# The last two recurrent steps of the last block, run in two halves of 256 positions with output rows beside the second half

## The chip, the cores and the metric

The kernel runs on one core of a Trainium2 chip. The metric is the device time of one execution in microseconds (us); the median of three runs before the change is 2809.48 us (2809.25 to 2809.84). Five engines work beside each other, each in the order of its own instruction list: PE multiplies matrices (PEld is its loading of weights), DVE, ACT and POOL work element by element, SP issues the DMA transfers. An engine whose next instruction waits does nothing else in the meantime.

## The reference

The input has 8 sequences of 2048 positions with 512 features. A long convolution with a residual comes first. Its result `x` then goes through a gated recurrence over the first axis: there are 8 steps, and the 2048 positions are the batch.

```
def step(c, xt):
    ft = sigmoid(xt @ wf.T + c @ uf.T + bf)
    it = sigmoid(xt @ wi.T + c @ ui.T + bi)
    gt = tanh(xt @ wc.T + c @ uc.T + bc)
    return ft * c + it * gt
c_final = scan(step, c0, x)                  # x: layer norm of the residual
h = tanh(x @ wo.T + c_final @ uo.T + bo)     # all 8 steps use the same c_final
out = x_residual + layernorm(h)
```

No output row of a position can be made before all 8 steps of that position are done, because `h` needs `c_final`. Different positions don't depend on each other.

## The kernel before, in words

**Tiles.** The 2048 positions are four blocks `q` of 512. A block is four chunks of 128 positions (`cj` 0 to 3). The products of a step are done by a scheme of Strassen's kind, with seven products of half blocks in place of eight: chunks 0 and 1 are one half of the positions, chunks 2 and 3 the other, and so a matmul has 256 moving columns (`BP`), of which the first 128 belong to chunks 0 and 2 and the last 128 to chunks 1 and 3. Numbers are split into a high and a low 16-bit part, and each product takes three matmuls.

**Units.** `part_a(key)` opens a unit: four accumulators of 256 columns in PSUM (pool `pu`, three buffers). It issues the products `FIRST` (24 matmuls with the input, then 24 with the state), and then ACT and DVE form sums of the accumulators in place (L993 to L997). `part_b(key)` adds the products `THEN` (18 and 18 matmuls), and ACT applies the gate's function (L1021). A step has two `z` units (the product of the input with `wo`, 24 and 18 matmuls, no state; stored to `z_d`, L1012 to L1014) and six gate units (three gates for each of two feature parts). All these matmuls are issued in `mms`, L955. When the third gate of a part is done, `state` (L1041 to L1047, DVE) makes the new state and `halves` (L1054 on ACT, L1056 on DVE) splits it into `cf`, which the next step's matmuls read.

**Order.** The order on each engine is written out by hand. A step is 16 places; its eight units go one after another, and each unit's closing part stands behind the opening part of the next. `put` files other work at places and `go` issues it there: `turn` reads the input rows of the next step, normalises them, transposes them on PE (L485) and splits them (L101, L102); `prep` makes the input of the next block; `head` makes the output rows of the block before, one every three places. A `head` loads `z` (a buffer of tag `zr`, of which there are four) and the residual row, adds the final product on POOL (L1128), applies tanh on ACT (L1131), takes statistics on DVE (L462 to L465), makes scale and offset by three small POOL instructions (L471 to L476), normalises on ACT (L1145), adds the residual on POOL (L1146) and stores. SP's list holds all loads and stores in the same hand-written order, so a load whose buffer is still in use holds up the ones behind it.

**The end.** The last block has no block after it. When its eighth step is done, the function `last` multiplies `c_final` with `uo` for its four chunks (`sums`, L450 to L452, 12, 12, 18 and 18 matmuls of 512 columns, two chunks in one PSUM tile) and adds the bias (L1098). Then 16 `tail` entries follow, each for one chunk and two steps: two additions on DVE (L1179), two tanh on ACT (L1180), statistics on DVE, the three small POOL instructions, two normalisations on ACT (L1187), and the residual additions on POOL (L1192; one in eight of them on DVE). Their loads reuse weight tiles and other tiles that the last step leaves.

Of the kernel before, what the change touches and what calls it, by code (L numbers as in the profile page):

```python
# [59 lines left out]
def s4_gated_block(ctx, tc, a, dbg=None):  # L60
# [888 lines left out]
    def mms(u, prods, w, x, opens, stop):  # L949
# [3 lines left out]
        for j, (f, b, d, k, i) in enumerate(n):  # L953
# [3 lines left out]
            seen.add(bank)  # L957

    def views(key):
        q, t, kind, n = key  # L960
        xf = xfs[q, t]
        if kind == "z":
            cs = slice(n * P, (n + 1) * P)
            return (lambda f, b, l, k: xf[:, b, int(l), k, cs], lambda f, b, l, k: wts[3][:, k, f, int(l)]), None
        ms = slice(n * P, (n + 1) * P)
        w, uw, cf = wts[kind], wts.get(4 + kind), cfs.get((q, t - 1))
        return ((lambda f, b, l, k: w[:, k, f, int(l), ms], lambda f, b, l, k: xf[:, b, int(l), k]),
                (lambda f, b, l, k: uw[:, k, f, int(l), ms], lambda f, b, l, k: cf[k][:, b, int(l)]))

# [4 lines left out]
    def part_a(key):  # L974

        q, t, kind, n = key
        z = kind == "z"
        u = units[key] = pu.tile([P, 4, BP], F32, name="u")
        for pr in FIRST:
            mms(u, places(key, pr), *views(key)[0], True, not t or z)  # L980
        if t and not z:
            mms(u, FIRST[0][:1] + FIRST[1] + FIRST[0][1:], *views(key)[1], False, True)
        if z:
            if n == 0:
                gates["z"] = FT.tile([P, 2, BP], F32, name="zc")
            c22 = gates["z"][:, n]
        else:
            g = gates[key] = FJ.tile([P, 4, BP], F32, name="gate2", tag="wq") if kind == 2 else FT.tile([P, 4, BP], F32, name=f"gate{kind}")
            c22 = g[:, 2]
        z_, v_ = (UV, UZ) if z else (UZ, UV)  # L990
        u2 = u2p[:, len(u2s) % 2]
        u2s.append(key)
        S.activation(u2, u[:, UX], AF.Copy)  # L993
        V.tensor_tensor(u2, u2, u[:, UY], ALU.add)  # L994
        V.tensor_tensor(c22, u2, u[:, z_], ALU.add)
        V.tensor_tensor(c22, c22, u[:, v_], ALU.add)
        V.tensor_tensor(u[:, 2:4], u[:, 2:4], u2[:, None].to_broadcast([P, 2, BP]), ALU.add)  # L997

    def part_b(key):

        q, t, kind, n = key
        u, z = units.pop(key), kind == "z"
# [22 lines left out]
        if kind == 2:  # L1025
            V.scalar_tensor_tensor(g, gates.pop((q, t, 1, n)), 1.0, g, ALU.add, ALU.mult)  # L1026
        elif kind == 0:
            return state(q, t, n)

    def state(q, t, n):  # L1030

        f, ig = gates.pop((q, t, 0, n)), gates.pop((q, t, 2, n))
        if t == 0:
            cds[q, n] = FT.tile([P, 4, BP], F32, name=f"cd{n}")
        cd = cds[q, n]
        for h in range(2):
# [12 lines left out]
        def halves():  # L1049
            cf = FT.tile([P, 7, 2, BP], F16, name=f"cf{n}", bufs=2 - n)  # L1050
            cfs.setdefault((q, t), []).append(cf)
            parts = ((0, cd[:, 0]), (slice(3, 5), ts[:, 0:2]), (slice(5, 7), ts[:, 2:4]), (slice(1, 3), cd[:, 2:4]))
            for fs, src in parts:
                S.activation(cf[:, fs, 0], src, AF.Copy)  # L1054
            for fs, src in parts:
                V.tensor_tensor(cf[:, fs, 1], src, cf[:, fs, 0], ALU.subtract)  # L1056
# [5 lines left out]
    def last(q):  # L1062
# [3 lines left out]
        def load():  # L1066
            if end:
                u4 = FE.tile([P, KT, 2, H], F16, name="uw", tag="xf")
                dma(out=u4, in_=uo_d.rearrange("k p a m -> p k a m"))
                uws.extend(u4[:, k] for k in range(KT))  # L1070
                return

            for i, (pool, tag) in enumerate(((FJ, "wl"), (FE, "y"))):
                u2 = pool.tile([P, 2, 2, H], F16, name="uw", tag=tag)
                dma(out=u2, in_=uo_d[2 * i : 2 * i + 2].rearrange("k p a m -> p k a m"))
                uws.extend(u2[:, k] for k in range(2))

        def load_b():
            bo = FE.tile([P, H], F32, name="bo", tag="xa", bufs=2) if end else FT.tile([P, H], F32, name="bo", tag="x1r", bufs=2)
            dma(out=bo, in_=a["bo"])  # L1080
            uws.append(bo)

        def sums(cj):
            cf, i, cs = cfs[q, NB - 1], cj // 2, slice(cj % 2 * P, (cj % 2 + 1) * P)
            if end and cj % 2:
                u = us[cj - 1]
            else:
                u = pu.tile([P, 4, BP], F32, name="u").rearrange("p (a b) c -> p a (b c)", a=2)
            us[cj] = u
            ps = [(k, b) for k in ((0, 2, 1, 3) if end else range(KT)) for b in (((FB11,) if i == 0 else (FB11, FT1)) if k < 2 else ((FB21,) if i == 0 else (FB22,)))]  # L1090
            for n, (k, b) in enumerate(ps):
                mm3(u[:, cj % 2], lambda l: cf[k % 2][:, b, l, cs], lambda l: uws[k][:, l],
                    start=(n == 0), stop=(n == len(ps) - 1))

        def out(cj):
            p_ = us[cj][:, cj % 2]
            if end:
                V.scalar_tensor_tensor(p_, uws[KT], SW, p_, ALU.mult, ALU.add)  # L1098
                us_[QC * q + cj] = p_
            else:  # L1100
# [15 lines left out]
    def head(q, cj, t):  # L1116
# [34 lines left out]
        return load, sum_, gate, stat, scale, load_x, out, store  # L1151

    def tail(q, cj, tp, n):

        c, s_ = QC * q + cj, {}

        def load():
            w = (3, 1, 5, 2, 6, 0)[n // 3]
            if n % 3 == 0:
                tails[w] = (FW if w < 2 else FV if w == 2 else FT).tile([P, 3, 2, H], F32, name="zz", tag=f"w{w}", bufs=1)  # L1160
            s_["z"] = tails[w][:, n % 3]
            dma(out=s_["z"], in_=z_d[c, :, 2 * tp : 2 * tp + 2])

        def load_x():
            i = (n + 3) % 9
            if n == 15:
                s_["x"] = tails[0][:, 1]
            elif i < 3:
                if i == 0:
                    tails[4] = FT.tile([P, 3, 2, H], F32, name="xw", tag="w4", bufs=1)  # L1170
                s_["x"] = tails[4][:, i]
            else:
                s_["x"] = (FJ, FJ, FE, FT, FJ, FT)[i - 3].tile([P, 2, H], F32, name="xx", tag=("wl", "ws", "y", "gate1", "wq", "gate0")[i - 3])
            dma(out=s_["x"], in_=x1_d[c, :, 2 * tp : 2 * tp + 2])
# [23 lines left out]

    tails = {}
    gsc = (0.5 / SW, 0.5 / SW, 1.0 / SW)  # L1200
    bias = FE.tile([P, 3, KT], F32, name="bias")
# [30 lines left out]
    end = last(NQB - 1)  # L1232
    rows = [tail(NQB - 1, cj, tp, 4 * cj + tp) for cj in range(QC) for tp in range(NB // 2)]

# [3 lines left out]
    for n, (q, t) in enumerate(steps):  # L1238
        b = 16 * n
        if q and t == 0:  # L1240
            put(last(q - 1), b, (-1, 4, 3, 5, 5, 7, 7, 9, 13, 14, 15))
        if n + 1 < len(steps):
            ps = ((2, 5, 6, 7, 8, 9), (9, 10, 11, 12, 13, 14)) if n else ((0, 1, 2, 3, 5, 6), (5, 6, 7, 8, 9, 10))
            for i in range(2):
                put(turn(*steps[n + 1], i), b, ps[i])
        if n == len(steps) - 1:
            put(end[:2], b, (2, 3))
            for i in range(3):
                put(rows[i][:2], b, (8 + 2 * i, 9 + 2 * i))
            for i in range(3, 9):  # L1250
                put(rows[i][:1], b, (13,))
        for (gp, cj), (n_, p) in zip(chunks, when):
            if n_ == n:
                put(prep(*pairs[gp], cj, (1, 0, 2)[cj] if n == 0 else 0), b, p)
        if q and t:
            for r in range(QC * NB):
                p = 3 * r + 17 - 16 * t
                if 0 <= p < 16:
                    put(head(q - 1, r // NB, r % NB), b, [p + d for d in (0, 2, 4, 6, 8, 9, 10, 12)])
    with tc.manual_schedule(engines=MAN | {mybir.EngineType.SP}):  # L1260
        before = None
        for n, (q, t) in enumerate(steps):
            zs = [(q, t, "z", i) for i in range(2)]
            gs = [(q, t, gt, mp) for mp in range(2) for gt in (1, 2, 0)]

            def finish(key, p):
                st_ = part_b(key)
                if st_:
                    put([st_], p, [1])

            for sl, key in enumerate(zs + gs if n else gs[:5] + zs + gs[5:]):
# [12 lines left out]
                go(p + 1)  # L1284
        part_b(before)
        for p in sorted(todo):
            go(p)
        for f in end[2:6]:
            f()
        for n in range(len(rows) + 5):  # L1290
            if n % 4 == 0 and n < len(rows):
                end[6 + n // 4]()
            for st_, d in ((0, -3), (1, -3), (6, 5), (2, 1), (3, 2), (4, 3), (5, 3)):
                if 0 <= n - d < len(rows) and (st_ > 1 or n - d > (2 if st_ else 8)):
                    rows[n - d][st_]()
# [62 lines left out]
```

## Time and profile before

| What | us |
|---|---|
| median of three runs | 2809.48 |
| profiled execution, its own time | 2808.14 |
| its span from first to last instruction | 2806.4 |
| PE busy in the span | 2552.5 (91%) |
| DVE busy | 2095.5 (75%) |
| ACT busy | 1480.0 (53%) |
| POOL busy | 1226.8 (44%) |
| last matmul of a gate issued, last block | 2724 |
| first statistics of a tail row | 2740.1 |
| last store issued | 2802.8 |

Busy shares are means over the whole span, in which stages with different limits follow each other: the convolution first, then four blocks of eight steps, then the tail. Where a row of the profile has a form such as `u<-xf,w`, the left side is the tile written and the right side the tiles read; `L955` is the line of the kernel that issued it. In a timeline the columns are start, duration, engine, line, operation, tiles, shape and how many instructions are merged. A chain of waits is read in order of time: each piece is what the next one was waiting for. PE works on several matmuls at once, so the time that matmuls take in a stream is the distance between their starts, not the duration shown for one.

### The profile page before, as it was taken

To read this page: it belongs to the slowest core of one execution; us is meant where nothing else is said; L and a number is where in the kernel's file an instruction comes from. 1 tells how busy PE (TensorE), PEld (TensorE's weight loads), DVE (VectorE), ACT (ScalarE), POOL (GpSimd) and SP (SyncE) were. 2 spreads that over 40 slices of the span, in tenths; PEclk is the share of its full clock that TensorE was granted. 3 is DMA by queue.
4 is the path that set the end of the run, shared out by engine and by line. 5 is a ranking of instruction groups with operands and counts; after the bars stand their busy time and mean duration, and the time that the engine had idled before them with its cause. 6 is when DMAs were issued, how large, how long until landed. Compare 5 with 4: busy or idle time off the path is not lost.

```text
span 2806.4 us, 60001 instructions
## 1 busy us (share of the span) xinstructions
PE 2552.5 (91%) x23940; PEld 2229.7 (79%) x23940; DVE 2095.5 (75%) x4248; ACT 1480.0 (53%) x3091; POOL 1226.8 (44%) x1520
## 2 busy tenths in 40 slices
PE   4578888896999999999999999999999999999991
PEld 3367777785888888788898887888898788888870
DVE  7878888867667766677887777778777677777748
ACT  8966666654444444445555444455555454554436
POOL 5777777743112211124554431355554224543307
PEclk9799999998999999999999999999999999999995
DMA  6977887887334433225564432356554234543356
GB/s 236 304 238 241 259 257 246 257 282 209 99 86 126 106 98 91 80 91 150 164 180 138 142 102 95 109 162 178 155 165 129 91 106 136 166 121 102 104 170 234
DMA packets 507536, 449.25 MB, mean 160 GB/s; under 512 B 275574, under 2 KB 386680, under 8 KB 502264
## 3 DMA queue, kind: packets, MB, share of 16 engines
q1 hardware_dynamic: 506824, 444.90, 52.7%
q8 instruction: 187, 3.06, 0.4%
q14 instruction: 93, 0.76, 0.1%
q10 hardware_dynamic: 432, 0.52, 0.1%
HBM read 293.58 MB, written 151.78 MB: 159 GB/s over the span
## 4 chain that ended last, share of the span: by engine, by line
PE 62%; DVE 7%; ACT 3%; issue 1%; POOL 1%; DMA 0%; SPq 0%; POOLq 0%; DVEq 0%; ACTq 0%
PE u L955 60%; PE pt L485 2%; DVE zz L1179 1%; ACT gate L1021 1%; DVE u L997 1%; DVE cd L1042 1%; DVE gate L1041 0%; DVE cf L1056 0%; DVE sth L462 0%; ACT xf L101 0%; DVE u2p L994 0%; DVE xf L102 0%; PE u L451 0%; ACT zr L1145 0%; ACT cf L1054 0%
## 5 line engine op out<-in xcount | busy, mean ns | idle before, releaser
L955 PEld LDWEIGHTS <-w 128*128 128x128 f16 x15120 | 1481.0, 98 | 198.9 <-issue 16.0
L955 PE MATMUL u<-xf,w 128*128 128x256 f16 x8064 | 944.2, 273 | 17.8 <-DVE u L997 6.1
L955 PE MATMUL u<-cf,w 128*128 128x256 f16 x7056 | 825.7, 273 | 2.0 <-DVE cf L1056 2.0
L1021 ACT ACTIVATE gate<-u,bias 128x512 f32<-128x512 f32 (+1 forms) x384 | 200.9, 574 | 275.2 <-PE u L955 274.9
L993 ACT ACTIVATE u2p<-u 128x256 f32<-128x256 f32 x256 | 96.6, 379 | 436.9 <-PE u L955 436.8
L955 PE MATMUL u<-w,xf 128*128 128x256 f16 x2688 | 310.5, 273 | 4.0 <-DVE u L997 4.0
L1146 POOL TENSOR_TENSOR x1r<-x1r,zr 128x512 f32<-128x512 f32 x96 | 133.4, 1390 | 410.5 <-ACT zr L1145 295.2
L994 DVE TENSOR_TENSOR u2p<-u2p,u 128x256 f32<-128x256 f32 x256 | 106.7, 417 | 267.3 <-ACT u2p L993 265.9
L909 POOL TENSOR_TENSOR xr<-y,xr 128x512 f32<-128x512 f32 x120 | 160.7, 1360 | 300.0 <-ACT y L908 300.0
L955 PEld LDWEIGHTS <-xf 128*128 128x128 f16 x2688 | 263.0, 98 | 36.3 <-DVE u L997 5.5
L997 DVE TENSOR_TENSOR u<-u,u2p 128x512 f32<-128x512 f32 x256 | 179.0, 699 | 8.7
L646 POOL TENSOR_TENSOR u<-xg,u 128x512 f16<-128x512 f32 x104 | 129.2, 1242 | 106.7 <-ACT u L644 105.6
L471 POOL TENSOR_TENSOR rsy<-rsy,nhalf 128x2 f32<-128x2 f32 (+1 forms) x68 | 51.0, 751 | 281.6 <-DVE rsy L465 280.6
L640 POOL TENSOR_TENSOR xg<-xg,mu 128x512 f32<-128x512 f32 x112 | 162.8, 1460 | 6.0 <-DMA xg<-in_xr 6.0
L102 DVE TENSOR_TENSOR x<-pxt,x 128x256 f16<-128x256 f32 x240 | 100.1, 419 | 63.6 <-ACT x L101 62.3
L1026 DVE SCALAR_TENSOR_TENSOR gate<-gate,gate 128x1024 f32<-128x1024 f32 x64 | 90.0, 1406 | 69.6 <-ACT gate L1021 68.5
L1128 POOL TENSOR_TENSOR zr<-zr,ur 128x512 f32<-128x512 f32 x96 | 130.0, 1354 | 21.1 <-DMA zr<-z_d 12.3
L666 PE MATMUL pxt<-x,at 128*128 128x256 f16 x224 | 61.9, 277 | 79.3 <-DVE x L102 78.9
L462 DVE BATCH_NORM_STATS2 sty<-y 128x6 f32<-128x512 f32 x120 | 76.9, 682 | 76.1 <-DMA y<-y_d 76.1
L101 ACT ACTIVATE x<-pxt 128x256 f16<-128x256 f32 x240 | 91.5, 382 | 73.5 <-PE pxt L666 67.8
L451 PE MATMUL pyt<-u,t 128*128 128x128 f16 (+2 forms) x544 | 123.7, 227 | 0.0
L452 PE MATMUL pyt<-u,t 128*128 128x128 f16 (+2 forms) x544 | 123.3, 227 | 0.0
(373 smaller groups left out, 5261.1 us busy)
## 6 DMA issues: line engine op xcount, KB each, us to landing
xs<-in_rr SPq DMA_DIRECT2D x32, 1024.0 KB, 6.4
t<-kpad SPq DMA_DIRECT2D x32, 1024.0 KB, 5.6
y_d<-y SPq DMA_DIRECT2D x30, 1024.0 KB, 7.6
xr<-in_r SPq DMA_DIRECT2D x60, 512.0 KB, 5.8
xa<-x_d SPq DMA_DIRECT2D x120, 256.0 KB, 4.0
y<-y_d SPq DMA_DIRECT2D x59, 512.0 KB, 5.8
x_d<-xr SPq DMA_DIRECT2D x59, 512.0 KB, 3.1
xg<-in_xr SPq DMA_DIRECT2D x28, 1024.0 KB, 8.6
```

Source lines behind the costliest of these rows:

```text
L102: V.tensor_tensor(lo, src, hi, ALU.subtract)
L451: T.matmul(out, lhsT=w(1), rhs=x(0), start=False, stop=False)
L452: T.matmul(out, lhsT=w(0), rhs=x(1), start=False, stop=stop)
L640: Q.tensor_tensor(xg, xg, bc(mu1), ALU.subtract)
L646: (V if g == 2 else Q).tensor_tensor(u[:, js, 1], xg, u[:, js, 0], ALU.subtract)
L909: Q.tensor_tensor(xv, yv, xv, ALU.add)
L955: T.matmul(u[:, d], lhsT=w(f, b, i == 1, k), rhs=x(f, b, i == 2, k), start=opens and bank not in seen, stop=stop and j == len(n) - 1, skip ...
L994: V.tensor_tensor(u2, u2, u[:, UY], ALU.add)
L997: V.tensor_tensor(u[:, 2:4], u[:, 2:4], u2[:, None].to_broadcast([P, 2, BP]), ALU.add)
L1021: act = lambda o, s_, b: S.activation(o, s_, AF.Tanh, scale=gsc[kind], bias=b)
L1128: Q.tensor_tensor(s_["z"], s_["z"], us_[c], ALU.add)
L1146: Q.tensor_tensor(s_["x"], s_["x"], s_["z"], ALU.add)
```

## The change

The six first steps of the last block, and everything before them, stay as they were, except for the places of the last `head` rows. For the last two steps (6 and 7):

- The gate units are split by columns into two halves of 128 (256 positions: chunks 0 and 2, then chunks 1 and 3). The order is step 6 of the first half, step 7 of the first half, step 6 of the second half, step 7 of the second half. The `z` units stay whole and stand at the four joints. A half unit has as many matmuls as a whole one, with 128 moving columns, and as many ACT and DVE instructions, on tiles half as wide.
- `part_a` is cut into `open_` (the input's matmuls) and `fill` (the state's matmuls and the sums). At three joints both first gate units are opened before the first is filled.
- The halves share `cf` tiles: the first half of step 6 writes a new tile for feature part 0 and the tile of step 5 for part 1, step 7 writes the tile of step 5.
- The output sums of chunks 0 and 2 stand in the second half's first step, and their result goes to SBUF (tile `ue`). Eight new `pair` entries make the output rows of these chunks beside the second half. They take `zr` buffers (two each; every third takes one tile `zp` instead), and sum and residual are added on POOL.
- Only the eight entries of chunks 1 and 3 remain in the `tail` after the last step. Their tiles, and those of `uw` and `bo`, are others than before.
- The `head` rows of the third block come every 2.5 places instead of every three.

```
+    def open_(key):
+        t, z = key[1], key[2] == "z"
+        u = units[key] = pu.tile([P, 4, BP], F32, name="u")[:, :, 0 : P if len(key) > 4 else BP]
+        for pr in FIRST:
+            mms(u, places(key, pr), *views(key)[0], True, not t or z)
+
+    def fill(key):
+        q, t, kind, n = key[:4]
+        z, u = kind == "z", units[key]
+        w = u.shape[-1]
         if t and not z:
             mms(u, FIRST[0][:1] + FIRST[1] + FIRST[0][1:], *views(key)[1], False, True)
...
+            if len(key) == 4 or t == NB - 2 and n == 0 and key[4] == 0:
+                cf = FT.tile([P, 7, 2, BP], F16, name=f"cf{n}", bufs=2 - n)
+            elif key[4] == 0:
+                cf = cfs[q, NB - 3][n]
+            else:
+                cf = cfs[q, t][n]
...
+    def pair(q, cj, tp, n):
+        c, s_ = QC * q + cj, {}
+
+        def load():
+            if n % 3 == 2:
+                z = FJ.tile([P, 2, H], F32, name="zp", tag="ws")
+                s_["z"] = [z[:, i] for i in range(2)]
+                dma(out=z, in_=z_d[c, :, 2 * tp : 2 * tp + 2])
+                return
+            s_["z"] = [FT.tile([P, H], F32, name="zr", bufs=4) for _ in range(2)]
+            for i in range(2):
+                dma(out=s_["z"][i], in_=z_d[c, :, 2 * tp + i])
+
+        def load_x():
+            s_["x"] = (FE, FJ)[n % 2].tile([P, 2, H], F32, name="xx", tag=("y", "wl")[n % 2])
+            dma(out=s_["x"], in_=x1_d[c, :, 2 * tp : 2 * tp + 2])
+
+        def sum_():
+            for z in s_["z"]:
+                Q.tensor_tensor(z, z, us_[c], ALU.add)
...
+        def out():
+            for i, z in enumerate(s_["z"]):
+                x = s_["x"][:, i]
+                Q.tensor_tensor(x, x, z, ALU.add)
...
-                p = 3 * r + 17 - 16 * t
+                p = (3 * r if q < NQB - 1 else (5 * r + 1) // 2) + 17 - 16 * t
...
+    SA, SB = 39, 47
+    put(end[:2], PL, (20, 30))
+    put((end[2], end[6]), PL, (SA, SA + 2))
+    put((end[4], end[8]), PL, (SB, SB + 1))
+    for i, r in enumerate(early_rows):
+        p0 = PL + SA + 3 + 3 * i
+        put(r, p0, ((-4 if i < 3 else -2), 0, 2, 3, 5, 3, 6, 7, 9))
+    for i, p in enumerate((50, 50, 50, 60, 60, 60, 61, 61)):
+        put(rows[i][:1], PL, (p,))
+    for i, p in enumerate((62, 61, 63, 63)):
+        put(rows[i][1:2], PL, (p,))
...
+        hs = [[(q, t, gt, mp, i) for mp in range(2) for gt in (1, 2, 0)] for i in range(2) for t in (NB - 2, NB - 1)]
+        zs = [(q, t, "z", i) for t in (NB - 2, NB - 1) for i in range(2)]
+        A, B = lambda k: [(part_a, k)], lambda k: [(finish, k)]
+        O, F = lambda k: [(open_, k)], lambda k: [(fill, k)]
+        run = lambda g: sum((A(g[k]) + B(g[k - 1]) for k in range(2, 6)), [])
+        first = lambda g: F(g[0]) + F(g[1]) + B(g[0])
+        two = lambda g: O(g[0]) + O(g[1])
+        plan = (A(zs[0]) + B(before) + A(zs[1]) + B(zs[0]) + two(hs[0]) + B(zs[1]) + first(hs[0]) + run(hs[0])
+                + A(zs[2]) + B(hs[0][5]) + B(zs[2]) + two(hs[1]) + first(hs[1]) + run(hs[1])
+                + A(hs[2][0]) + B(hs[1][5]) + A(hs[2][1]) + B(hs[2][0]) + run(hs[2])
+                + A(zs[3]) + B(hs[2][5]) + B(zs[3]) + two(hs[3]) + first(hs[3]) + run(hs[3]) + B(hs[3][5]))
+        for p, (f, key) in enumerate(plan):
+            f(key, PL + p) if f is finish else f(key)
+            go(PL + p)
```

In the list that `put` gets for a `pair`, the numbers are the places of load of `z`, sum, tanh, statistics, small POOL group, load of the residual, normalisation, residual addition and store, counted from the pair's own place; the places now are the 63 entries of `plan`, each some half as long as a place before. Input rows of step 7 (`turn`) stand at entries 1 to 17.

## The prediction

> **What bounds the kernel now.** I read the windows of the last 150 us first, then the chain that ended last, then the timeline at the places that the change touches. All times are microseconds from the span's start. First the windows (columns: stretch, length, busy time and count of PE, PEld, DVE, ACT, POOL, granted clock, DMA share, GB/s):
>
> ```profile
> 2440.00:2502.80 62.80, 62.80 (x578) 56.48 (x576) 49.47 (x98) 32.66 (x65) 30.92 (x42) 1.00 0.59 166
> ...
> 2660.00:2724.00 64.00, 64.00 (x589) 57.37 (x587) 33.57 (x63) 19.58 (x41) 8.86 (x14) 1.00 0.50 166
> 2724.00:2740.00 16.00, 11.80 (x42) 4.25 (x41) 9.37 (x16) 4.84 (x9) 0.00 (x0) 0.79 0.54 193
> 2740.00:2790.80 50.80, 4.68 (x22) 1.94 (x20) 49.60 (x106) 35.64 (x55) 42.57 (x62) 0.59 0.70 230
> 2790.80:2806.00 15.20, 0.00 (x0) 0.00 (x0) 6.60 (x12) 5.15 (x8) 11.46 (x14) 0.50 0.66 267
> ```
>
> Up to 2724 PE has no gap and everything else hides under it. From 2740 DVE is the bound (49.60 of 50.80) and POOL is close (42.57). The chain says the same, with the hand-over between:
>
> ```profile
> 2646.91 77.30 PE u L955 x708
> ...
> 2724.24 0.70 ACT gate L1021
> ...
> 2731.55 0.61 PE u L451
> ...
> 2736.95 0.71 DVE u L1098
> ...
> 2740.17 0.66 DVE sth L462 x2
> ...
> 2790.84 0.66 DVE sth L462 x2
> ```
>
> The reader is to see three prices: last gate matmul to first statistics 16 us; then one output pair after another, (2790.84 - 2740.17)/14 = 3.62 us each; then 15.6 us from the fifteenth pair's statistics to the end. So tail from first statistics to end is 2806.4 - 2740.1 = 66.3 us for 16 pairs. Of the last two steps, the first matmul (z unit of step 6) starts at 2590.0, which is where I start the sum.
>
> **The change, part by part.**
>
> *Tail.* Eight of 16 pairs leave it: 66.3 - 8 x 3.62 = 37.3 us from first statistics to the end. Gross gain 29 us. All else is what this costs.
>
> *Narrow matmuls.* 24 half units of 84 matmuls (2016, 128 moving columns) replace 12 units (1008, 256 columns at 109 ns, from 578 matmuls in 62.8 us). Nearest rows, convolution stage:
>
> ```profile
> 303.11 0.22 PE L450 MATMUL pyt<-u,t 128*128 128x128 f16 x1
> 303.16 0.23 PE L451 MATMUL pyt<-u,t 128*128 128x128 f16 x1
> 303.23 0.23 PE L452 MATMUL pyt<-u,t 128*128 128x128 f16 x1
> 303.29 0.22 PE L450 MATMUL pyt<-x,m 128*128 128x120 f16 x1
> 303.34 0.22 PE L451 MATMUL pyt<-x,m 128*128 128x120 f16 x1
> 303.39 0.22 PE L452 MATMUL pyt<-x,m 128*128 128x120 f16 x1
> ```
>
> Starts lie 50 to 70 ns apart for 128 columns with strided weights (mean 62; weight load 150 ns) and 52.5 ns for 120 columns with dense weights (weight load 98 ns, as in the gates). I scale the second to 128 columns: 56 ns, so 2016 x 56 - 1008 x 109 = +3 us; ends 0 (54.5 ns) and +15 (62 ns). The Trainium skill ("TensorE: Matmul & The Clock Gate", Back-to-back issue gap) gives about 81 ns for a sustained load-and-multiply pair at 128 columns; by that the estimate would be 2016 x 81 - 1008 x 109 = +53 us and the kernel 50 us slower than my sum. The rows above contradict it, and I go by them.
>
> *PE up to slot 42.* I call an entry of the new plan a slot (0 to 62). The first early pair's sum stands at slot 42. PE work from 2590.0 to there: closing part of the unit before 36 x 0.109 = 3.9; three z units 3 x 42 x 0.109 = 13.7; twelve half units 12 x 84 x 0.056 = 56.4; 300 of the 504 matmuls of the next half step, 300 x 0.056 = 16.8; two transposes of 0.87 = 1.7; output sums of chunk 0, 12 x 0.2155 = 2.6. Sum 95.2.
>
> *Waits that the change adds on PE there.* Order and cover change at the start of step 6. The second z unit closed after a full 5.2 us opening of the next gate; now only two half openings (2.7 us) stand ahead of it. What it waits for is DVE:
>
> ```profile
> 2603.30 0.68 DVE L1056 TENSOR_TENSOR cf<-cd,cf 128x512 f16<-128x512 f32 x1
> 2603.90 0.41 DVE L994 TENSOR_TENSOR u2p<-u2p,u 128x256 f32<-128x256 f32 x1
> ...
> 2605.26 0.70 DVE L997 TENSOR_TENSOR u<-u,u2p 128x512 f32<-128x512 f32 x1
> ```
>
> DVE is on the state and its halves until 2603.98, so that z unit's sums end at 2605.96, while PE would be there at 2603.8. The second opening takes the first z unit's PSUM buffer (three in all), which ACT empties only after the state's copies, about 2605.1. That is 2.6 us of idle PE. Behind it: statistics, POOL's three small instructions (1.2) and two norms (1.5) must come ahead of the moved transposes, and ACT's first copy of the next unit is queued behind them: 1.9 us more. At the next step boundary DVE has 2.3 us of input halves ahead of the z sums: 1.8 us. Sum 6.5 us; ends 0 (all other boundaries of the trace show none) and 10. SP's next input loads wait for the transposes, 20 us ahead of need. The remaining half units wait little: per half step DVE has 17.7 us (128-column operations at 0.28, 256 at 0.42, 512 at 0.69) against 27.5 us of PE, and the state chain of about 4.1 us is covered by 4.6 us of z and openings. No half unit waits for the other half's state in the compiled order. So slot 42 starts at 2590.0 + 95.2 + 6.5 = 2691.7.
>
> *Early pairs.* Each takes two sums and two outs on POOL, 1.28 each (row L1128 shows 1.35 in the mean), a small group of 1.2, two tanh and two norms on ACT, 2.25 of statistics on DVE, and on SP one or two z loads, an x load and a store. Slot 42 to the first out: units 2.7 + 2.0 + 2.7 + 2.0, z and a closing 2.6 + 2.0, sums of chunk 2 3.9, z closing 2.0, copies and norm 1.9: 21.8 us. From there a ring binds. The z buffers hold three pairs, so the load of pair i+3 waits in SP's queue for the out of pair i; its sum on POOL waits for that landing; and on POOL the out of pair i+1 stands behind that sum. One turn is out 2.55, issue 0.1, landing, sum 2.6. Landings:
>
> ```profile
> xa<-x_d SPq DMA_DIRECT2D x120, 256.0 KB, 4.0
> ...
> zr<-z_d SPq DMA_DIRECT2D x96, 256.0 KB, 4.4
> ...
> zz<-z_d SPq DMA_DIRECT2D x16, 512.0 KB, 6.2
> ```
>
> Five turns (outs 0 to 4, sums 3 to 7), one of them with a 512 KB load: 5 x 5.25 + 4 x 4.4 + 6.2 = 50.0. Ends: windows of 50 us show medians of 3.1 (xa) to 5.6 (zr) and 4.6 (xx) to 6.4, so 43 to 55. Pitch would be 10 us against 6 planned, and DVE has 43 us of work in PE's 48 us from slot 42 to 62, so nothing is caught up. While a sum is late, its tanh blocks ACT, and with it the gate copies, the state and PE (I find PE idle for some 9 us here, last gate matmul about 2749). That is no term: the ring ends later than PE.
>
> *Ring to tail.* Remaining pairs end ahead of the late ones on every queue. After the last sum: out 2.55, small group 1.2, norm 0.8, out 2.55, small group 1.2, two norms 1.6, then the late row's tanh 0.6, plus 1 for an x load behind a store: 11.5. Last output sums (24 matmuls, 0.43 cold or 0.22, about 8 us) and chunk 1's out on DVE lie beside that. Ends 8 (x early) and 14.
>
> *At no cost.* Uw and bo move to tiles that are free by then, and load 20 slots ahead of their use. The heads of the block before come every 2.5 slots instead of 3 in steps 25 to 29: PE is full there and DVE has 49.5 of 62.8, so some 2 us more of DVE a step hide; if not, 1 us a step. DVE and ACT have 78 and 64 more instructions in the compiled order, POOL 18, SP 6, all counted above. Late z loads are issued before PE ends, as now.
>
> *Sum.* 2590.0 + 101.7 + 21.8 + 50.0 + 11.5 + 37.3 = 2812.3, against 2806.4: +5.9 us. The profiled execution took 2808.14, the median of the three runs 2809.48; with the same distance from span to median (3.1), 2815.
>
> **The rivals.**
>
> *The ring turns faster and the tail's gain stays (faster).* Place: the landing between an out and the sum three pairs on. With 3.1 and 4.6 us five turns take 43.3, and without the 6.5 us of boundary waits the end is at 2799.1; with the landings fully hidden, POOL alone needs 5 x (5.15 + 1.2) = 32, end 2788 to 2794. It decides from an average landing of 3.6 us (five turns in 44 us) with boundary waits as summed, or 4.9 us without them. For it: landings of 3.7 in 2600 to 2660. Against: early loads, stores and late loads together move some 20 MB in 75 us, about the rate of the tail now, where 512 KB take 5.3 to 8.1.
>
> *PE is dearer than thought (slower).* 62 ns up to slot 42 adds 1308 x 6 ns = 8, boundary waits of 10 add 3.5, and a gap near 3 us halves the granted clock (0.50 at 2730 to 2734, spacing 0.43 in place of 0.2155) for some 4 us: 2. End 2820 to 2828.
>
> *The halves don't separate:* both write one cf tile, and units of the second half could wait for the first half's state, 4 us at each of two places, end 2820. The compiled order has no such wait; I give it no chance of its own.
>
> **How the numbers follow.** About 0.2% (5.6 us) is what a measurement can tell from no change. Forecast 0.5, its own range 2802 to 2828: half of it beyond +5.6, 0.07 of the case below -5.6, the rest within. Faster ring 0.26, median 2791 to 2806, nine tenths of it beyond -5.6. Dearer PE 0.24, all slower. Faster 0.035 + 0.235 = 0.27, same 0.215 + 0.025 = 0.24, slower 0.25 + 0.24 = 0.49. The range drops a tenth on each side: 2797 to 2829.
>
> **What would show it.** Starts of 128-column gate matmuls 56 ns apart; PE idle 2 to 3 us near 2603; the first early sum near 2696; sums three pairs on waiting for z DMAs, with a pitch near 10 us; ACT's early tanh waiting for POOL; first late statistics near 2775 and 37 us from there to the end. Wrong if the early sums keep a pitch of 6 to 7 us, or if PE ends last and the tail starts on its sums.

## The result and the profile after

The changed kernel takes 2836.23 us (median of five runs, 2833.03 to 2836.88) against 2809.37 us (2807.24 to 2809.84) before. The ratio is 1.0094, with a 95% interval from 1.0079 to 1.0108: 27 us slower. The prediction said 2815, with a range up to 2829. The profiled execution has a span of 2830.9 us, against 2806.4 before.

First the windows of the kernel after (stretch, length, busy time and count of PE, PEld, DVE, ACT, POOL, granted clock, DMA share, GB/s):

```profile
2440.00:2502.80 62.80, 54.31 (x475) 47.12 (x473) 43.39 (x91) 29.45 (x58) 31.60 (x43) 0.97 0.53 156
...
2724.00:2750.00 26.00, 22.28 (x391) 21.94 (x389) 11.97 (x36) 13.24 (x29) 13.27 (x15) 1.00 0.59 188
2750.00:2780.00 30.00, 19.86 (x150) 13.00 (x149) 24.87 (x52) 14.22 (x33) 21.99 (x24) 0.77 0.73 254
2780.00:2830.90 50.90, 0.00 (x0) 0.00 (x0) 30.74 (x60) 23.88 (x36) 33.40 (x48) 0.52 0.59 209
```

The first row is the surprise. This stretch lies some 100 us ahead of the two steps that the change is about, and PE, which was busy for all of its 62.80 us, now idles for 8.5 of them. Step 6 starts at 2599.50 instead of 2589.98. The other rows show the end: with the early pairs running, no engine is full, neither beside PE nor after it.

Then what PE waited for: rows with idle time from the timeline of PE after (the bracket is the idle time ahead of the row and what ended it):

```profile
2498.39 1.78 PE L485 MATMUL pt<-cst,xa 128*128 128x128 f32 x8 [4.24 <-ACT xa L941]
...
2614.33 1.93 PE L955 MATMUL u<-xf,w 128*128 128x128 f16 x24 [2.19 <-ACT zt L1023]
...
2651.92 3.23 PE L955 MATMUL u<-w,xf 128*128 128x256 f16 x18 [2.12 <-DVE u L1012]
...
2750.53 1.62 PE L955 MATMUL u<-xf,w 128*128 128x128 f16 x24 [3.78 <-ACT gate L1036]
...
2756.97 1.18 PE L955 MATMUL u<-xf,w 128*128 128x128 f16 x18 [2.26 <-DVE u L1012]
...
2763.18 2.10 PE L955 MATMUL u<-xf,w 128*128 128x128 f16 x18 [4.02 <-DVE u L1012]
```

The first row belongs to the stall ahead of step 6: the transposes of a step's input come late, because their rows (`xa`) were normalised late. The 2.19 and 2.12 are the two joints that the prediction had summed as 2.6 and 1.8. The last three are the interference of the early pairs: without the pairs (experiment 6) these waits are not there.

How the rows came late in the first row can be read from SP's and POOL's timelines (L1152 is the load of a head's z, L1168 that of its residual row, L1173 the out that adds it):

```profile
2484.80 0.32 SPq L1152 DMA_DIRECT2D zr<-z_d  x1
...
2488.78 0.39 SPq L1168 DMA_DIRECT2D x1r<-x_d  x1
...
2493.83 1.26 POOL L1173 TENSOR_TENSOR x1r<-x1r,zr 128x512 f32<-128x512 f32 x1 [4.67 <-issue]
```

SP stands at the z load until POOL has done the out that frees its buffer; the residual row, which is loaded one place ahead of its out, comes only after that, and POOL idles for 4.67 us ahead of the out that needs this row. The trace names no releaser here; the out's other input, normalised on ACT (L1172), was ready at 2487.9. Behind that out, on POOL, stand the small instructions that ACT's normalisation of `xa` waits for.

And the chain that ended last, in order of time, after 2700 (SPq is SP's own queue; pieces of issue time up to 0.1 us are left out):

```profile
2704.65 14.17 PE u L955 x228
...
2733.50 7.57 DMA out<-xx
2741.09 0.32 SPq L1196
2741.51 4.84 DMA zr<-z_d
2746.43 0.69 POOL zr L1200
...
2749.48 0.76 ACT gate L1036 x2
...
2756.91 4.90 DVE cf L1080 x4
...
2772.42 10.06 DMA out<-xx
2782.50 0.32 SPq L1196
...
2783.86 7.21 DMA out<-xx
2791.13 4.76 DMA xx<-x_d
2796.01 2.48 POOL xx L1219 x2
```

Three landings of early stores (`out<-xx`: 7.57, 10.06 and 7.21 us) lie on it. Each time SP stands at an x load (L1196), whose buffer is one of two and is still being stored; at 2741.51 the z load that the next sum waits for stands behind it as well. The prediction had 1 us for this.

The span by landmarks, each kernel's profiled execution:

| | before | after | forecast |
|---|---|---|---|
| start of step 6 | 2590.0 | 2599.5 | 2590.0 |
| from there to slot 42 | | 105.2 | 101.7 |
| slot 42 to first early out | | 22.2 | 21.8 |
| first early out to the end of the last early sum | | 50.1 | 50.0 |
| from there to the first late statistics | | 15.4 | 11.5 |
| first late (tail) statistics to the end | 66.3 | 38.6 | 37.3 |

### The profile page after: what moved, and what is told of

Read it like the earlier page. It is cut to its first block, busy times and chain, and to the rows that moved or that the text cites. A ratio compares the mean times of both kernels' runs of the same rounds, so it can differ in the third digit from the quotient of the medians.

```text
span 2830.9 us, 62175 instructions
## 1 busy us (share of the span) xinstructions
PE 2563.6 (91%) x24948; PEld 2248.1 (79%) x24948; DVE 2108.6 (74%) x4326; ACT 1489.7 (53%) x3155; POOL 1249.3 (44%) x1538
## 4 chain that ended last, share of the span: by engine, by line
PE 58%; DVE 7%; ACT 3%; DMA 3%; POOL 2%; issue 2%; SPq 1%; POOLq 0%; DVEq 0%; ACTq 0%
PE u L955 55%; PE pt L485 2%; DVE cf L1080 1%; DMA out<-xx 1%; ACT gate L1036 1%; DVE u L1012 1%; DVE cd L1059 1%; ACT xf L101 1%; DVE gate L1058 1%; DVE xf L102 1%; DMA y<-y_d 0%; DMA x1r<-x_d 0%; DVE u2p L1009 0%; POOL xr L909 0%; POOL x1r L1173 0%
## 5 line engine op out<-in xcount | busy, mean ns | idle before, releaser
L955 PEld LDWEIGHTS <-w 128*128 128x128 f16 x16128 | 1499.7, 98 | 208.9 <-issue 24.3
L955 PE MATMUL u<-xf,w 128*128 128x256 f16 (+1 forms) x8568 | 951.2, 267 | 35.8 <-DVE u L1012 16.8
L955 PE MATMUL u<-cf,w 128*128 128x256 f16 (+1 forms) x7560 | 832.9, 266 | 2.8 <-DVE cf L1080 2.8
L1036 ACT ACTIVATE gate<-u,bias 128x256 f32<-128x256 f32 (+2 forms) x408 | 205.7, 555 | 262.1 <-PE u L955 261.7
L1008 ACT ACTIVATE u2p<-u 128x256 f32<-128x256 f32 (+1 forms) x268 | 98.6, 368 | 423.3 <-PE u L955 423.2
L1009 DVE TENSOR_TENSOR u2p<-u2p,u 128x256 f32<-128x256 f32 (+1 forms) x268 | 108.5, 405 | 261.6 <-ACT u2p L1008 260.2
L1173 POOL TENSOR_TENSOR x1r<-x1r,zr 128x512 f32<-128x512 f32 x96 | 133.0, 1385 | 379.3 <-ACT zr L1172 242.1
L909 POOL TENSOR_TENSOR xr<-y,xr 128x512 f32<-128x512 f32 x120 | 160.3, 1357 | 290.5 <-ACT y L908 290.5
L1012 DVE TENSOR_TENSOR u<-u,u2p 128x512 f32<-128x512 f32 (+1 forms) x268 | 181.0, 675 | 9.2
L102 DVE TENSOR_TENSOR x<-pxt,x 128x256 f16<-128x256 f32 x240 | 100.0, 418 | 64.1 <-ACT x L101 62.8
L1041 DVE SCALAR_TENSOR_TENSOR gate<-gate,gate 128x1024 f32<-128x1024 f32 (+1 forms) x68 | 90.5, 1331 | 68.5 <-ACT gate L1036 67.4
```

Source lines behind the costliest of these rows:

```text
L102: V.tensor_tensor(lo, src, hi, ALU.subtract)
L909: Q.tensor_tensor(xv, yv, xv, ALU.add)
L955: T.matmul(u[:, d], lhsT=w(f, b, i == 1, k), rhs=x(f, b, i == 2, k), start=opens and bank not in seen, stop=stop and j == len(n) - 1, skip ...
L1036: act = lambda o, s_, b: S.activation(o, s_, AF.Tanh, scale=gsc[kind], bias=b)
L1173: Q.tensor_tensor(s_["x"], s_["x"], s_["z"], ALU.add)
```

## The experiments

All times are medians; the kernel before had 2810.11, 2810.71, 2810.38 and 2810.47 us in the four groups. Single executions of one kernel lie up to 4.6 us from its median, so verdicts go by medians and ratios, and the profiles are read for what waits for what.

**1. The heads alone** (kernel before, one line changed)

```
- p = 3 * r + 17 - 16 * t
+ p = (3 * r if q < NQB - 1 else (5 * r + 1) // 2) + 17 - 16 * t
```

> The kernel before with one part of the change alone: the output rows of the block before (heads) come every 2.5 places instead of every 3. Theory 1 (no slack): a head's z buffer is one of four, its load stands ten places ahead of its out, and four times 2.5 is ten, so the load of head r+4 stands in SP's queue at the very place where the out of head r is still to come; SP waits there, the loads and stores of the inputs behind it come late, and PE stalls while the input rows (prep) still run. Step 6 would then start at 2598 to 2600 instead of 2590 and the kernel take 2817 to 2820 us. Theory 2 (load): the extra work of a fifth more heads a step on DVE, ACT and POOL is too much; the same time, but the waits would be on DVE or ACT with SP not waiting for POOL. Theory 3: the 9.5 us before step 6 come from another part of the change; then 2809.

Measured: 2818.57 us, ratio 1.0027 [1.0016, 1.0038]. With nothing else of the change, the kernel is 8 us slower. In the profiled execution, the fastest of seven (2814.02 us), step 6 starts at 2596.45, and PE idles 5.2 us between 2440 and 2502.80. The waits of SP's queue between 2400 and 2510 (who waits, for whom, total us, times, longest); in the kernel before, of those for a head:

```profile
SPq L1149 <- POOL x1r L1146: 29.1, 5, 13.8
```

and the same view with the denser heads:

```profile
SPq L1125 <- POOL x1r L1146: 45.3, 9, 10.0
SPq L1123 <- POOL zr L1128: 5.8, 1, 5.8
```

L1125 is the load of a head's z, L1146 the out of a head, L1149 its store. Before, SP waits mostly at stores (another 35.9 us at those of the input rows, L916), and PE stays full all the same; with the denser heads it waits nine times at a z load, for the out that frees its buffer.

**2. The life of a head's buffer shortened** (changed kernel)

```
- ps = [b + p + d for d in (0, 2, 4, 6, 8, 9, 10, 12)]
+ ps = [b + p + d for d in ((0, 2, 4, 6, 8, 9, 10, 12) if q < NQB - 1 else (0, 2, 3, 5, 6, 7, 8, 10))]
```

> The changed kernel, heads every 2.5 places as there, but the life of a head's z buffer cut from ten places to eight (sum at 2, tanh at 3, statistics 5, scale 6, x load 7, out 8, store 10), which gives the buffer back its two places of slack. Theory 1 (no slack): step 6 starts at 2590 to 2592 and the kernel takes 2827 us (9 us less than the changed kernel). Theory 2 (load): the same work in the same places, so 2836 as the changed kernel.

Measured: 2832.01 us, 1.0080 [1.0065, 1.0095]: some 4 us gained (the intervals of the two kernels overlap) where one theory said 9 and the other none. Step 6 started at 2596.39. No z load of a head stood among SP's eight longest waits any more, but the steps of a head now lay closer together, and the largest totals (same view, 2370 to 2500) were others:

```profile
SPq L916 <- POOL xr L909: 41.4, 5, 11.7
SPq L1176 <- POOL x1r L1173: 19.6, 6, 5.8
```

L916 is the store of an input row, L909 its sum on POOL. This edit changed two things at once, the slack and the order, and so did not settle it.

**3. The dense heads after the last input rows** (changed kernel)

```
- p = (3 * r if q < NQB - 1 else (5 * r + 1) // 2) + 17 - 16 * t
+ p = (3 * r if q < NQB - 1 or r < 20 else (5 * r + 21) // 2) + 17 - 16 * t
```

> The changed kernel with the first twenty heads every 3 places and the rest every 2.5, so that the dense ones come after the last input rows (prep) and the last three heads stand in the plan of the last two steps. Theory 1: with no prep behind them in SP's queue the dense heads cost nothing, step 6 starts at 2590 to 2592; 2827 us, or up to 2 more where the heads in the plan disturb it. If dense heads stall PE without prep as well, step 6 starts 3 to 5 us late and the time is 2831.

Measured: 2825.35 us, 1.0057 [1.0042, 1.0072], 11 us better than the changed kernel; step 6 started at 2588.64, and PE was full from 2440 to 2585, beside the first dense heads too. Heads every 2.5 places cost nothing where no input rows of a block stand beside them.

**4. A fifth z buffer, with the heads alone** (the kernel of experiment 1; the same at every tile of tag `zr`)

```
- FT.tile([P, H], F32, name="zr", bufs=4)
+ FT.tile([P, H], F32, name="zr", bufs=5)
```

> The kernel before with heads every 2.5 places (8 us slower than the kernel before) and, for the heads, five z buffers in place of four, nothing else. Theory 1 (no slack in the z buffers): a load of a head now waits for the out of the head five before, which stands 2.5 places ahead of it; SP waits no longer, and the time is that of the kernel before, 2809 to 2812. Theory 2 (load: more head work on DVE, ACT and POOL beside the last input rows): nothing changes, 2816 to 2820.

Measured: 2811.78 us, 1.0001 [0.9992, 1.0011]: no difference from the kernel before. The work of the heads is the same, in the same places, on the same engines. What differs is that a load no longer waits for an out at its own place: none of SP's waits of over 1 us between 2400 and 2510 is at a z load. PE still lost 3.6 us there in the profiled execution, which did not show in the time. What held it is not shown; the load theory is one candidate, and the load of the next chunk's product (L1123), at which SP waits 10.1 us for POOL, another:

```profile
2440.00:2502.80 62.80, 59.23 (x537) 52.29 (x535) 48.25 (x100) 32.40 (x64) 35.64 (x52) 1.00 0.66 190
```

**5. A fifth z buffer in the changed kernel** (the same edit)

> The changed kernel with five z buffers of 256 KB in place of four (for heads and early pairs alike), nothing else. By the no-slack theory the 9.5 us before step 6 go and the rest stays: step 6 starts at 2590 to 2591, time 2826 to 2828. If the early pairs gain as well from the fifth buffer (half a pair more ahead in the ring), up to 5 us more: 2821. If the loss before step 6 had another cause in this kernel than in the kernel before with the heads alone: 2836.

Measured: 2825.51 us, 1.0053 [1.0037, 1.0068], 10.7 us less than the changed kernel, the first of the three cases. In the profiled execution step 6 starts at 2593.38, not yet at 2590 to 2591, and PE idles 2.3 us of the stretch instead of 8.5. The row of SP's waits (2400 to 2510) that carried the loss, in the kernel after:

```profile
SPq L1152 <- POOL x1r L1173: 48.4, 8, 9.9
```

It is missing from the same view with five buffers, where these are among the longest (L1168 is the load of a head's residual row, which has two buffers):

```profile
SPq L916 <- POOL xr L909: 20.4, 3, 7.7
SPq L1168 <- DMA out<-x1r: 10.5, 7, 3.6
```

So the cause of the loss ahead of step 6 is shown from both sides by the times: alone it makes the kernel before slower, and one more buffer takes it away in both kernels. The profiles of single executions agree in part: 2 to 4 us of idle PE stay there with five buffers, and without any stall step 6 starts anywhere from 2588.64 to 2593.14 (experiments 3 and 7), so that the 9.5 us of the profile are themselves known to a few us.

**6. Without the early pairs** (changed kernel; rows of chunks 0 and 2 left out)

```
  for i, r in enumerate(early_rows):
      p0 = PL + SA + 3 + 3 * i
-     put(r, p0, ((-4 if i < 3 else -2), 0, 2, 3, 5, 3, 6, 7, 9))
+     pass
```

> The changed kernel with the eight early pairs left out (chunks 0 and 2 of the last block's output rows are not written; their output sums on PE stay). It measures what the early pairs cost PE. Theory A (the pairs hold PE up: ACT stands at a tanh whose sum waits for a z landing, and gates, state and PE behind it): without them the half units run with the boundary waits only, last gate matmul 142 us of PE work and 8 of waits after the start of step 6, at 2749 instead of 2767; first late statistics 16 us later, then 38 us of tail: 2803 and a time of 2808. Theory B (the half units hold each other up: ACT and DVE can't follow operations on 128 positions): last gate matmul stays at 2762 or later, time 2820.

Measured: 2805.49 us, 0.9986 [0.9976, 0.9995], with the heads' loss still in it. The last gate matmul ends 48.8 us after slot 42 (62.5 in the kernel after), and the first late statistics come 13.6 us after that (25.2). From the timelines of PE and DVE of this kernel:

```profile
2705.11 1.50 PE L955 MATMUL u<-xf,w 128*128 128x128 f16 x24 [0.82 <-ACT gate L1036]
...
2752.74 1.17 PE L955 MATMUL u<-cf,w 128*128 128x128 f16 x18
...
2767.54 1.28 DVE L462 BATCH_NORM_STATS2 sth<-zz 128x6 f32<-128x512 f32 x2
```

Theory A holds: the half units themselves run about as forecast (last gate matmul 152 us after the start of step 6, 150 expected), and the pairs hold PE up by 14 us. This kernel also gives an account of the change, from one execution of each kernel. From the start of step 6 to the first late statistics it takes 165.9 us against 150.1 before: the half units, the joints and the output sums moved ahead cost 15.8. The pairs add 27.0 (192.9 in the kernel after). They take 27.7 off the tail (66.3 to 38.6). So the pairs just about pay for themselves, and the loss is what is left: 15 us of halves, and the 9.5 us ahead of step 6.

**7. Out ahead of the sum; a third x buffer; both** (all three on the kernel of experiment 3)

```
- put(r, p0, ((-4 if i < 3 else -2), 0, 2, 3, 5, 3, 6, 7, 9))
+ put(r, p0, (-4, 0, 2, 3, 4, 3, 5, 5, 7))
```

> The kernel with the dense heads late (2825 us), and one thing more: on POOL the out of early pair i+1 stands ahead of the sum of pair i+3 instead of behind it, so that the z landing lies beside an out and a small group. Theory R (the ring out, z load, landing, sum, out sets the pitch of the early pairs): the pitch falls from 10 us to the next limit, which is x (store landing, x load landing and an out for two pairs, about 8 us a pair) or POOL's own 6.4 us; first late statistics 8 to 15 us earlier, time 2810 to 2817. Theory D (the early pairs are held by DVE, which has 43 us of work in 48, or by the DMA rate): the pitch stays at 10 and the time at 2823 to 2827.

```
- s_["x"] = (FE, FJ)[n % 2].tile([P, 2, H], F32, name="xx", tag=("y", "wl")[n % 2])
+ if n % 3 == 2:
+     s_["x"] = [FT.tile([P, H], F32, name="x1r", bufs=2) for _ in range(2)]
...
+ x = s_["xx"] = (FE, FJ)[n % 3].tile([P, 2, H], F32, name="xx", tag=("y", "wl")[n % 3])
```

> The kernel with the dense heads late (2825 us), with a third buffer for the x rows of the early pairs (the two that the heads have left) in place of two, nothing else. Theory X (after the ring the last two pairs wait for x loads that stand in SP's queue behind stores): the stretch from the last early sum to the first late statistics falls from 15 us to about 11.5 and the time to 2821; the ring keeps its pitch of 10 us. Theory R alone says 2825, as nothing in the ring changes.

> Both edits: out ahead of the sum, and the third x buffer. If the ring and then the x buffers set the early pairs' pitch, both gone leaves POOL with 6.4 us a pair, PE is held up less, and the early pairs end before PE does: late statistics start some 14 us after the last gate matmul, at 2755 to 2762, and the kernel takes 2795 to 2803, faster than before. If something else holds the pairs (DVE, the DMA rate), 2820 or more.

| | us | ratio |
|---|---|---|
| neither (experiment 3) | 2825.35 | 1.0057 [1.0042, 1.0072] |
| out ahead | 2824.15 | 1.0050 [1.0034, 1.0067] |
| third x buffer | 2818.50 | 1.0030 [1.0019, 1.0041] |
| both | 2822.43 | 1.0044 [1.0029, 1.0059] |

The third x buffer gains 7 us, more than the 4 expected: the stretch from the last early sum to the first late statistics fell from 15.7 to 12.5 us in the profiles, and the tail behind it from 38.4 to 36.4. The theory of stores in the way holds. Both edits together are no better than the third buffer alone (the intervals overlap), and nothing of the 2795 to 2803 came.

The ring theory does not hold as it stood. With the out ahead, no early sum waits for a z landing any more, and yet the sums keep their pitch: from the third (2718.15) to the eighth (2771.47) it is 10.7 us. The timeline of ACT in this kernel (out ahead), at the gate that PE waited for until 2747.48:

```profile
2737.37 0.28 ACT L1008 ACTIVATE u2p<-u 128x128 f32<-128x128 f32 x1 [1.95 <-PE u L955]
2743.97 1.52 ACT L1214 ACTIVATE zr<-zr,nmh,rsh 128x512 f32<-128x512 f32 x2 [6.32 <-POOL nmh L476]
2745.39 1.13 ACT L1204 ACTIVATE zr<-zr 128x512 f32<-128x512 f32 x2
2746.43 0.39 ACT L1036 ACTIVATE gate<-gate,bias 128x128 f32<-128x128 f32 x1
```

and in the kernel after, where the z landing made POOL late:

```profile
2740.08 0.28 ACT L1008 ACTIVATE u2p<-u 128x128 f32<-128x128 f32 x1
2747.72 0.63 ACT L1204 ACTIVATE zr<-zr 128x512 f32<-128x512 f32 x1 [7.36 <-POOL zr L1200]
2748.94 0.63 ACT L1204 ACTIVATE zr<-zr 128x512 f32<-128x512 f32 x1 [0.59 <-POOL zr L1200]
2749.48 0.39 ACT L1036 ACTIVATE gate<-gate,bias 128x128 f32<-128x128 f32 x1
```

The picture is the same: a gate's tanh (L1036) stands behind an early pair's tanh or norm that waits 6 to 7 us for POOL, and PE waits for the gate. Only the reason why POOL is late has changed. The pairs are filed at slots of PE's plan, so when PE stands, the slots stretch and the pairs with them. That this coupling alone sets the pitch is not shown: DVE and the DMA rate, the other theories, got no experiment of their own, and the last section shows DVE slowed beside POOL.

**8. Five early pairs every four slots, three rows of chunk 2 first among the late ones** (on the kernel with the third x buffer)

```
- p0 = PL + SA + 3 + 3 * i
- put(r, p0, ((-4 if i < 3 else -2), 0, 2, 3, 5, 3, 6, 7, 9))
+ p0 = PL + SA + 3 + 4 * i
+ put(r, p0, (-4, 0, 3, 4, 5, 3, 7, 8, 10))
...
+ NE = 5
+ list_ = [(cj, tp) for cj in (0, 2, 1, 3) for tp in range(NB // 2)]
+ early_rows = [pair(NQB - 1, cj, tp, i) for i, (cj, tp) in enumerate(list_[:NE])]
+ rows = [tail(NQB - 1, cj, tp, i) for i, (cj, tp) in enumerate(list_[NE:])]
...
```

The tiles and places of the eleven late rows change with it.

> The kernel with dense heads late and the third x buffer (2818 us), with five early pairs every 4 slots instead of eight every 3, tanh and norm one slot later behind the POOL work that they wait for; the three other pairs of chunk 2 become the first late ones, whose output sums are long done, so that the late pairs start under the output sums of chunks 1 and 3. Theory C (coupling: at 3 slots a pair POOL is 90% full, so ACT, which also serves the gates, stands at tanh and norm, PE stands behind ACT, and the slots that time the pairs get longer): PE is no longer held up, last gate matmul 47 us after slot 42 as without early pairs, first late statistics 6 to 9 us after it, then 48 us of tail for 11 pairs: end 2797 to 2800, time 2800 to 2804, 0.2 to 0.4% faster than before. If instead the DMA rate or the half units themselves hold PE and the pairs, last gate matmul stays 54 us or more after slot 42 and the time is 2810 or more.

Measured: 2813.03 us, 1.0008 [0.9999, 1.0016]. Gates no longer stand behind a pair's tanh, and the last gate matmul ends 53 us after slot 42 instead of 61 (third x buffer). The expectation said 47; most of the rest is PE waiting for DVE's sums of the gates (1.45, 1.15 and 1.95 us in PE's timeline), among which the pairs' statistics stand. The first late statistics came 10.8 us after the last gate, not 6 to 9, because the first late tanh stood on ACT behind the norm of the last early pair, which waited 4.62 us for POOL. The theory of coupling is borne out for ACT, though number, spacing and places of the pairs change at once and which of them did it is open; the version comes out level with the kernel before.

**9. Three waits of that version** (sums of the first two late pairs, halves of step 5, inputs of step 7)

```
+ for i, p in enumerate((62, 63)):
+     put(rows[i][2:3], PL, (p,))
...
- put([st_], p, [1])
+ put([st_], p, [2 if p == PL + 1 else 1])
...
- for i, ps in enumerate(((1, 2, 4, 5, 7, 9), (8, 9, 11, 13, 15, 17))):
+ for i, ps in enumerate(((1, 2, 4, 5, 7, 9), (6, 7, 9, 11, 13, 15))):
```

> The kernel with five early pairs every 4 slots (2813 us) with three moves in its order: the sums and tanh of the first two late pairs stand ahead of the last early pair's norm instead of behind its wait for POOL (4 us of the start of the late pairs); the halves of the last state of step 5 one slot later, behind the copies that free the first z unit's PSUM buffer (2.2 us of idle PE at the start of step 6); and the second part of step 7's inputs two slots earlier, ahead of the z unit that waited 2.8 us for its sums behind them. If these three waits are what they look like, each on the path, the kernel takes 2804 to 2807 us, 0.1 to 0.2% faster than before; if DVE and POOL, both nearly full from the last gate on, take the gain back, 2810 or more.

Measured: 2812.81 us, 1.0006 [0.9997, 1.0015]: nothing gained. The wait of 2.19 us for ACT's `zt` copies stayed as it was, but its theory was not tested, as the second edit moved nothing. The unit that closes at that place is the last one of step 5, of feature part 1, and for that part `state` issues the halves at once and gives `put` nothing to place. The timeline of ACT shows them (L1078) ahead of the `zt` copies still, in the order that the version of experiment 8 has:

```profile
2604.28 0.61 ACT L1078 ACTIVATE cf<-cd 128x512 f16<-128x512 f32 x1
2604.80 0.36 ACT L1008 ACTIVATE u2p<-u 128x256 f32<-128x256 f32 x1
2605.07 0.80 ACT L1172 ACTIVATE zr<-zr,nmh,rsh 128x512 f32<-128x512 f32 x1
2605.78 0.37 ACT L1022 ACTIVATE zt<-u 128x256 f32<-128x256 f32 x1
```

The wait of the z unit of step 7 (2.83 us in experiment 8) went, and one for the norm of a head came 3 us ahead of it. From the timeline of PE:

```profile
2606.68 1.50 PE L955 MATMUL u<-xf,w 128*128 128x128 f16 x24 [2.19 <-ACT zt L1023]
...
2641.78 1.18 PE L955 MATMUL u<-xf,w 128*128 128x128 f16 x18 [2.00 <-ACT zr L1172]
```

The late statistics started 8.5 us after the last gate instead of 10.8, and the tail behind them was longer by 1.7 (51.1 against 49.4). So one move had no effect, and the other two moved waits without a gain. No version was found that beats the kernel before.

## Why the prediction was wrong

By its own terms, on the profiled execution: 2812.3 forecast, +9.5 (start of step 6), +3.4 (to slot 42), +0.4 (first out), +0.1 (ring), +3.9 (ring to tail), +1.3 (tail) make 2830.9. To the median come 5.3 us in place of 3.1.

- **The step that failed: "At no cost", the heads.** It said that PE is full and DVE has 49.5 of 62.8, so the denser heads hide, "if not, 1 us a step". They cost 9.5 us in the profile, and in the medians 8 in experiment 1 and 10.7 in experiment 5. I asked whether the engines had time, and not whether the buffers and SP's queue had. The numbers lay in the code: four buffers, one load every 2.5 places, ten places from load to out. Four times 2.5 is ten, so each load stood at the place of the out that it needs, and what stands behind it in SP's list came late: in the longest stall the next head's residual row, with POOL, ACT's normalisation of the input rows and PE's transposes waiting in turn. At 3 places the same buffers had two places to spare. Moving the heads moves their loads as well; that needed a term in the sum and a rival of its own, and the prediction's rivals are all about the two steps themselves.
- **The term that was mis-sized: "Ring to tail", 11.5 with 1 us for an x load behind a store.** It took 15.4. The x loads of the last two pairs waited for stores that took 10.06 and 7.21 us to land. A store's landing had been priced in no row of the sum. (The last output sums beside this stretch are 30 matmuls, 12 and 18, and not 24; they entered no sum.)
- **PE up to slot 42**: 105.2 for 101.7. The matmuls came as forecast: units of 84 start 4.69 us apart in steady running (2677.62, 2682.31, 2687.00), 55.8 ns each, against 56 forecast. The two large waits were 2.19 and 2.12 us for 2.6 and 1.8; of the 1.9 us summed between them 0.20 came, and all idle time of PE in the stretch is 5.8 us. (The three recorded waits add up to 6.3, not 6.5.) What the sum had no term for was the clock: 0.95 granted from 2590 to 2660, where the kernel before has 1.00, by an estimate 3.5 us of 70. It was 0.67 from 2616 to 2620, behind the gap of 2.19 us, and 0.60 from 2652 to 2656, behind that of 2.12. The prediction had a halved clock only in a rival, behind a gap near 3 us. In the execution of experiment 5 the same gaps (2.19 and 2.11) left the clock at 1.00, and the stretch took 103.5.
- **The ring**: 50.1 us for 50.0, and the pitch as forecast, but the mechanism only in part. In the longest turn the z load stood behind an x load that waited for a store, and with the landings taken out of the ring the pitch stayed (experiment 7). What the prediction named as no term, that a late sum "blocks ACT, and with it the gate copies, the state and PE", is the other half of the loop, since the pairs' places are slots of PE's plan. The right number there was luck as far as its one cause goes.
- **Tail**: 38.6 for 37.3, right.
- **Rivals**: the faster ring did not come, and PE was not dearer by its narrow matmuls. Neither had anything to do with the miss. Without the two mis-priced terms (experiments 3 and 7, third x buffer) the kernel takes 2818.5, near the forecast.

The Trainium skill ("TensorE: Matmul & The Clock Gate", Back-to-back issue gap) gives some 81 ns for a sustained pair of weight load and matmul at 128 columns. The runs show 55.8 ns over a whole half step, and the rows of the convolution had been the better guide.

## What to carry to other kernels

When entries that repeat are put closer together, multiply spacing by buffers and compare with the life of a buffer from load to last use; if nothing is left over, every load in the in-order DMA queue becomes a wait for compute, and all behind it comes late, however idle the engines look. Count stores the same way: a buffer is in use until its store has landed, here up to 10 us. And where filler work is threaded through an engine that also serves the critical one, taking away one of its waits can gain little (the out ahead, in experiment 7, gained 1 us of 2825) while another blocking entry stands ahead of the critical work.

## What the runs showed of the hardware

DVE's operations with both inputs in SBUF took about three times as long while POOL was adding. From the timeline of DVE of the kernel after, while POOL adds without a pause from 2756.18 to 2761.54:

```profile
2756.48 0.43 DVE L1012 TENSOR_TENSOR u<-u,u2p 128x256 f32<-128x256 f32 x1
2756.82 0.77 DVE L1080 TENSOR_TENSOR cf<-cd,cf 128x128 f16<-128x128 f32 x1
2757.52 2.90 DVE L1080 TENSOR_TENSOR cf<-gate,cf 128x256 f16<-128x256 f32 x2
2760.34 1.48 DVE L1080 TENSOR_TENSOR cf<-cd,cf 128x256 f16<-128x256 f32 x1
```

and the same instructions of an earlier unit in the same kernel, with POOL idle:

```profile
2690.42 0.28 DVE L1080 TENSOR_TENSOR cf<-cd,cf 128x128 f16<-128x128 f32 x1
2690.62 0.79 DVE L1080 TENSOR_TENSOR cf<-gate,cf 128x256 f16<-128x256 f32 x2
2691.33 0.42 DVE L1080 TENSOR_TENSOR cf<-cd,cf 128x256 f16<-128x256 f32 x1
```

One of 256 columns takes 1.45 to 1.48 us instead of 0.40 to 0.42, a little more than one POOL addition (1.25 to 1.28). L1012, which reads `u` in PSUM, keeps its 0.43. POOL is slowed as well: its two additions from 2758.69 take 2.85 us instead of 2.49. The four L1080 instructions took 4.9 us instead of 1.3. They lie on the chain that ended last, ahead of the sums for which PE waits 4.02 us at 2763.18. The prediction had no term for this, as it counted DVE's and POOL's work as if they ran beside each other freely.

The Trainium skill ("SBUF — State Buffer", SBUF: two separate sides) says that DVE and GpSimd share one pair of ports, which one instruction holds for its whole length, on DVE's side also one with two SBUF inputs. These rows agree with it.
